# Gate rows spread over four turns and between other pieces, and channel means broadcast by a DMA through DRAM, in a two-layer graph attention kernel

## The chip, the cores and the metric

The kernel runs on one core of one Trainium2 chip. The metric is device time in microseconds (us) of one execution; a kernel's time is the median of its runs. The profile is one execution, recorded by the hardware profiler. Engines are named as the profile does: PE is TensorE, PEld its weight loads, DVE is VectorE, ACT is ScalarE, POOL is GpSimd, SP the queue that issues the DMAs.

## The reference, cut to what matters

Two layers on x of shape (16, 1024, 256). The first (a graph convolution with two batch norms) is untouched by the change. In the second, every one of the 16 batches needs this:

```python
fea = jnp.transpose(x, (0, 2, 1))                       # x: (16, 1024, 256)
c_adj = jnp.mean(fea, axis=1)                           # channel means, one per node: (16, 1024)
diff = c_adj[:, None, :] - c_adj[:, :, None]            # 1024 x 1024 per batch
A = jnp.abs(jnp.abs(jax.nn.sigmoid(diff) - 0.5) - 0.5) * 2.0
A_s = (A + jnp.transpose(A, (0, 2, 1))) * 0.5
Wg = adj[None, :, :] * A_s                              # the gate, times the adjacency matrix
g = jnp.einsum('bcn,bnm->bcm', fea, Wg)
g = jax.nn.relu(g * para.reshape(1, C, N))              # becomes the queries, 4 heads of 64
# k, v = x @ kv_w ; attention = softmax(q k^T * scale) v ; then a residual and a layer norm
```

A *gate row* in the kernel is 128 of the 1024 rows of Wg, for all 1024 columns: eight gate rows, 0 to 7, per batch. To make one, ScalarE needs the means of all 1024 nodes along the free axis, the same in every partition. That tile is called `crow`.

## The kernel before: the parts that matter

The attention phase is a software pipeline over batches. While batch b-1 is in attention, the keys, values, gate rows and graph product of batch b are made, and the input of batch b+1 is normalised. One batch of attention is eight *turns*; a turn has two steps of scores, exponentials and attention matmuls, and a list of other pieces of work. `at` says which pieces belong to a turn, and `arrange` puts them in order. Every engine works in its program order.

```python
ps_s = pool("ps_s", 2, space=PSUM)     # PSUM holds TensorE's results; scores: two tiles
ps_t = pool("ps_t", 3, space=PSUM)     # everything else: three tiles
...
def crow(b, h):                        # the means of a batch, spread over all partitions, in two halves
    if h == 0:
        crows[b] = crp.tile([P, N], F32, tag="crow", name=f"crow_{b}")
    p = ps_t.tile([P, FB], F32, tag="t", name="pc")
    for k in range(FB // P):
        j = h * (FB // P) + k
        nc.tensor.transpose(p[:, ts(k, P)], css[b][:, j : j + 1].to_broadcast([P, P]), ident)
    nc.scalar.copy(crows[b][:, ts(h, FB)], p)

def wg_a(b, i):                        # gate row i: an odd one is one ScalarE pass, an even one two
    t = wgp.tile([P, N], F32, tag="wg", name=f"wg_{b}_{i}")
    wgs[b, i] = t
    if i % 2:
        nc.scalar.activation(t, crows[b], AF.Tanh, bias=hcs[b][:, i : i + 1], scale=-0.5)
        ti = t.bitcast(mybir.dt.int32)
        nc.vector.tensor_scalar(ti, ti, -(2**31), None, op0=OP.bitwise_or)
    else:
        nc.scalar.activation(t, crows[b], AF.Abs, bias=css[b][:, i : i + 1], scale=-1.0)
        nc.scalar.activation(t, t, AF.Tanh, scale=-0.5)

def wg_b(b, i):                        # VectorE: times the adjacency row
    t = wgs[b, i]
    nc.vector.scalar_tensor_tensor(t, t, 1.0, adj_sb[:, i, :], op0=OP.add, op1=OP.mult)
...
WG = (3, 3, 1, 1)                      # gate rows made in turns one to four
...
def arrange(pieces):
    few = sorted((fa for fa in pieces if fa[0] not in long), key=lambda fa: rank.get(fa[0], 11))
    many = [fa for fa in pieces if fa[0] in long]        # keys, values, graph: TensorE's long pieces
    ...                                                  # gate rows have the last rank: they stand together,
                                                         # behind the turn's other short pieces
for t in ...:                          # one turn (cut)
    scores(g + 2); exps(g + 2)
    ...
    sums(g)                            # VectorE adds up the exponentials, for the softmax denominators
    for f, a in now:                   # the turn's other pieces, arranged
        f(*a)
    sums(g + 1)
    scores(g + 3); exps(g + 3)
    attend(g); attend(g + 1)
```

Two more pieces recur below. `finish_a` transposes an output block into a tile `pf` of the pool `ps_t`, and VectorE reads it into a tile `r`, which frees the PSUM tile; that product is "r" in what follows. `values` makes the value projection into a tile `pv` of the same pool.

## Time and profile before

| what | before |
|---|---|
| median of the first three runs (range) | 2753.9 us (2753.35 to 2755.53) |
| a steady batch of the attention phase | 113.03 us |
| TensorE busy in it | 111.25 us |
| ScalarE, VectorE busy in it | 62.17 us, 70.83 us |

One view more: VectorE's order. The columns are start (us), length (us), engine, line, operation, output and inputs, count, and in brackets idle time before and its releaser.

```profile
1353.45 2.48 DVE L521 TENSOR_TENSOR acc<-acc,e 128x1024 f32<-128x1024 f32 x2
1355.84 1.22 DVE L518 TENSOR_TENSOR acc<-e,e 128x1024 f32<-128x1024 f32 x1
1356.98 0.68 DVE L574 TENSOR_TENSOR r<-pf,RD 128x512 f32<-128x512 f32 x1
```

Three additions for the denominators (`acc`, 3.7 us together) stand directly ahead of r, the product that frees the PSUM tile for which a value projection waits until 1357.71.

### The profile page before, as it was taken

The numbers are of one execution on the slowest core, as the hardware profiler recorded it, in microseconds if no ns is written. First come the engines' busy times: TensorE is split into PE (matmuls) and PEld (weight loads), VectorE is DVE, ScalarE is ACT, GpSimd is POOL, SyncE is SP. The second block draws the span as 40 slices with busy tenths as digits, with TensorE's granted clock in tenths as the row PEclk, the third lists the DMA queues.
The fourth block names the chain that finished last, engine by engine and source line by source line (L and its number), as shares of the span: only waits on it lengthen the run. The fifth ranks groups of instructions, "written<-read, shape, count | busy, mean of one in ns | idle before, by whom it ended". The sixth has DMA issues, their size and how long they took to land.

```text
span 2752.7 us, 24565 instructions
## 1 busy us (share of the span) xinstructions
PE 2684.0 (98%) x9306; PEld 1153.1 (42%) x9306; DVE 1305.4 (47%) x2089; ACT 1249.2 (45%) x1695; POOL 184.4 (7%) x404
## 2 busy tenths in 40 slices
PE   8999999999999799999999999999999999999997
PEld 4444444444444443444434444444443444444432
DVE  3101101102222555657656566565665756656646
ACT  2111111112555554654645546456464564645634
POOL 0000000000000100001001010010100100001002
PEclk9999999999999899999999999999999999999999
DMA  3212212220682200000100001000100011000000
GB/s 122 77 62 91 80 59 90 82 86 0 212 298 100 89 24 27 24 23 27 43 24 24 23 28 43 23 23 28 38 28 24 24 35 35 24 24 27 12 8 25
DMA packets 90524, 146.89 MB, mean 53 GB/s; under 512 B 7200, under 2 KB 73248, under 8 KB 84256
## 3 DMA queue, kind: packets, MB, share of 16 engines
q1 hardware_dynamic: 90400, 145.26, 15.0%
q8 instruction: 75, 1.23, 0.2%
q14 instruction: 49, 0.40, 0.0%
HBM read 86.52 MB, written 58.72 MB: 53 GB/s over the span
## 4 chain that ended last, share of the span: by engine, by line
PE 90%; DVE 5%; ACT 3%; issue 1%; DMA 0%; POOL 0%; SPq 0%; DVEq 0%; ACTq 0%; POOLq 0%
PE pa L215 16%; PE s L500 16%; PE pg L480 16%; PE o L530 15%; PE po L304 8%; PE ph L228 8%; PE pk L454 4%; PE pv L465 3%; DVE wg L446 1%; PE px L413 1%; PE pd L549 1%; PE py L390 1%; PE pf L571 1%; DVE acc L521 1%; PE pr L560 1%
## 5 line engine op out<-in xcount | busy, mean ns | idle before, releaser
L512 ACT ACTIVATE e<-s 128x1024 f32<-128x1024 f32 x512 | 497.4, 1020 | 599.7 <-PE o L530 351.8
L500 PE MATMUL s<-qT,kT 64*128 64x512 f32 x2048 | 509.7, 616 | 17.4 <-ACT e L512 17.4
L521 DVE TENSOR_TENSOR acc<-acc,e 128x1024 f32<-128x1024 f32 x384 | 469.5, 1223 | 18.6
L480 PE MATMUL pg<-wg,x 128*128 128x512 f32 x1024 | 470.4, 593 | 0.6 <-DVE wg L446 0.6
L530 PE MATMUL o<-e,v 128*64 128x512 f32 x2048 | 467.7, 599 | 0.0
L215 PE MATMUL pa<-AhT,x 128*128 128x512 f32 x1024 | 442.0, 592 | 0.5 <-issue 0.5
L247 DVE BATCH_NORM_STATS2 st<-ph 128x6 f32<-128x512 f32 x128 | 89.4, 698 | 558.6 <-ACT hT L246 558.6
L500 PEld LDWEIGHTS s<-qT,kT 64*128 64x128 f32 x2048 | 175.0, 186 | 327.0 <-issue 192.1
L215 PEld LDWEIGHTS pa<-AhT,x 128*128 128x128 f32 x1024 | 194.7, 190 | 244.9 <-issue 243.7
L530 PEld LDWEIGHTS o<-e,v 128*64 128x64 f32 x2048 | 135.6, 136 | 316.4 <-issue 315.3
L480 PEld LDWEIGHTS pg<-wg,x 128*128 128x128 f32 x1024 | 180.4, 191 | 160.4 <-issue 159.0
L228 PE MATMUL ph<-agg,W1T 128*128 128x512 f32 x512 | 222.2, 592 | 0.0
L222 ACT COPY agg<-pa 128x512 f32<-128x512 f32 x64 | 37.4, 585 | 404.7 <-PE pa L215 404.7
L446 DVE SCALAR_TENSOR_TENSOR wg<-wg,adj_sb 128x1024 f32<-128x1024 f32 x128 | 156.8, 1225 | 77.5 <-ACT wg L442 74.0
L304 PE MATMUL po<-hL,W2T 128*128 128x512 f32 x384 | 165.0, 592 | 0.0
L518 DVE TENSOR_TENSOR acc<-e,e 128x1024 f32<-128x1024 f32 x64 | 78.2, 1221 | 153.1 <-PE pd L549 153.1
L228 PEld LDWEIGHTS ph<-agg,W1T 128*128 128x128 f32 x512 | 97.4, 190 | 122.3 <-issue 122.1
L485 DVE TENSOR_TENSOR qT<-pg,para_sb 128x512 f32<-128x512 f32 x64 | 44.2, 690 | 204.3 <-PE pg L480 204.3
L246 ACT COPY hT<-ph 128x512 f32<-128x512 f32 x128 | 74.9, 585 | 144.9 <-PE ph L228 144.9
L465 PE MATMUL pv<-kvw,x1T 128*128 128x256 f32 x512 | 119.4, 382 | 6.6 <-DVE r L574 6.6
L308 DVE BATCH_NORM_STATS2 st<-po 128x6 f32<-128x512 f32 x64 | 44.7, 698 | 169.4 <-PE po L304 169.4
L454 PE MATMUL pk<-x1T,kvw 128*128 128x512 f32 x256 | 117.3, 601 | 1.0 <-ACT kT L457 1.0
(106 smaller groups left out, 1990.6 us busy)
## 6 DMA issues: line engine op xcount, KB each, us to landing
h<-hT SPq DMA_DIRECT2D x24, 1024.0 KB, 3.8
hL<-h SPq DMA_DIRECT2D x24, 1024.0 KB, 6.3
x<-in_x_dram SPq DMA_DIRECT2D x16, 1024.0 KB, 5.1
yT<-y SPq DMA_DIRECT2D x32, 512.0 KB, 3.7
yt<-yT SPq DMA_DIRECT2D x64, 256.0 KB, 3.5
xr<-in_x_dram SPq DMA_DIRECT2D x64, 256.0 KB, 3.6
out_dram<-r SPq DMA_DIRECT2D x64, 256.0 KB, 2.1
A<-in_adj_dram SPq DMA_DIRECT2D x4, 1024.0 KB, 8.1
```

The source lines that it names most:

```text
L215: nc.tensor.matmul(p, xts[b][:, k, ts(c, P)], AhT[:, k, ts(h, FB)], start=(k == 0), stop=(k == NT - 1),)
L228: nc.tensor.matmul(p, W1T[:, k, ts(f, P)], aggT[b][:, k, ts(h, FB)], start=(k == 0), stop=(k == CT - 1),)
L247: nc.vector.bn_stats(st1[:, f, u, :], p)
L304: nc.tensor.matmul(po[c], W2T[:, k, ts(c, P)], hT[u][:, k, :], start=(k == 0), stop=(k == HT - 1))
L446: nc.vector.scalar_tensor_tensor(t, t, 1.0, adj_sb[:, i, :], op0=OP.add, op1=OP.mult)
L454: nc.tensor.matmul(p, kvw[:, k, ts(c, P)], x1Ts[b][:, k, ts(h, FB)], start=(k == 0), stop=(k == CT - 1))
L465: nc.tensor.matmul(p[:, ts(a, C)], x1Ts[b][:, k, ts(j + a, P)], kvw[:, k, C:], start=(k == 0), stop=(k == CT - 1),)
L480: nc.tensor.matmul(pg[b], x1s[b, k // 2][:, k % 2, ts(c, P)], wgs[b, k][:, ts(h, FB)], start=(k == 0), stop=(k == NT - 1))
L500: nc.tensor.matmul(t[:, h, :], kTs[b, pair][h * HD : (h + 1) * HD, ts(cb, P)], qTs[b, pair, hf][h * HD : (h + 1) * HD, :], start=True, sto ...
L512: nc.scalar.activation(E[g, a], S.pop((g, a)), AF.Exp)
L521: nc.vector.tensor_add(ACC[b, hf, pair], ACC[b, hf, pair], E[g, a])
L530: nc.tensor.matmul(O[b, hf, pair][h * HD : (h + 1) * HD, :], vs[b][:, cb, pair * P + h * HD : pair * P + (h + 1) * HD], E[g, a][:, h, :], ...
```

## The change

Its intent is threefold. First, seven of a batch's eight broadcast transposes leave TensorE: one transpose, a 4 KB store and a DMA that reads the stored row into all 128 partitions do the same. Second, gate rows are made two per turn. Third, they no longer stand in one block but row by row (a row is a pair of pieces, `wg_a` and `wg_b`) between others. The rest of `arrange` also moves other pieces: in the second turn the pf transposes go behind the first value projection. The core of the diff:

```diff
+    c_dram = [dram.tile([NT, P], F32, name=f"crow_d{b}") for b in range(B)]
-        def crow(b, h):
+        def crow(b):
             ...                                    # batch 0 keeps the eight transposes
+            nc.tensor.transpose(p[:NT, :P], css[b], ident)
+            t = crows[b][:NT, :P]
+            nc.scalar.copy(t, p[:NT, :P])
+            nc.sync.dma_start(c_dram[b], t)
+            nc.sync.dma_start(crows[b], c_dram[b].rearrange("j p -> (j p)").partition_broadcast(P))
-        WG = (3, 3, 1, 1)
+        WG = (2, 2, 2, 2)
         def arrange(pieces):
+            first = [fa for fa in pieces if fa[0] is dens]
+            gate = [fa for fa in pieces if fa[0] in (wg_a, wg_b)]
             ...                                    # "order": the other pieces, short between long
+            pairs = [gate[k : k + 2] for k in range(0, len(gate), 2)]
+            res = spread(order, pairs) if order else pairs
             ...
+            return first + flat
```

More of the change, by code (lines that the diff above doesn't have):

```diff
@@ L419, in means @@
             nc.vector.tensor_scalar_mul(hcs[b], css[b], 0.5)
-        def crow(b, h):
-            if h == 0:
-                crows[b] = crp.tile([P, N], F32, tag="crow", name=f"crow_{b}")
-            p = ps_t.tile([P, FB], F32, tag="t", name="pc")
-            for k in range(FB // P):
-                j = h * (FB // P) + k
-                nc.tensor.transpose(p[:, ts(k, P)], css[b][:, j : j + 1].to_broadcast([P, P]), ident)
-            nc.scalar.copy(crows[b][:, ts(h, FB)], p)
+        def crow(b):
+            crows[b] = crp.tile([P, N], F32, tag="crow", name=f"crow_{b}")
+            if b == 0:
+                for h in range(NH):
+                    p = ps_t.tile([P, FB], F32, tag="t", name="pc")
+                    for k in range(FB // P):
+                        j = h * (FB // P) + k
+                        nc.tensor.transpose(p[:, ts(k, P)], css[b][:, j : j + 1].to_broadcast([P, P]), ident)
+                    nc.scalar.copy(crows[b][:, ts(h, FB)], p)
+                return
+            p = ps_t.tile([P, FB], F32, tag="t", name="pc")
+            nc.tensor.transpose(p[:NT, :P], css[b], ident)
[3 more added lines that the diff above has]
+            nc.sync.dma_start(crows[b], c_dram[b].rearrange("j p -> (j p)").partition_broadcast(P))
         def wg_a(b, i):
@@ L653, in fast @@
             put(b - 2, NC - 2, means, b)
-            for h in range(NH):
-                put(b - 2, NC - 1, crow, b, h)
+            put(b - 2, NC - 1, crow, b)
             i = 0
@@ L683, in fast, with spread @@
         long = (keys, values, graph)
+        def spread(few, many):
+            res, done = [], 0
+            for k, fa in enumerate(few):
+                upto = len(many) * (k + 1) // (len(few) + 1)
+                res += many[done:upto] + [fa]
+                done = upto
+            return res + many[done:]
         def arrange(pieces):
-            few = sorted((fa for fa in pieces if fa[0] not in long), key=lambda fa: rank.get(fa[0], 11))
+            first = [fa for fa in pieces if fa[0] is dens]
+            gate = [fa for fa in pieces if fa[0] in (wg_a, wg_b)]
             many = [fa for fa in pieces if fa[0] in long]
-            n = sum(f in short for f, _ in few)
-            res, k, done = [], 0, 0
-            for f, a in few:
-                res.append((f, a))
-                if f in short and f is not dens:
-                    k += 1
-                    upto = len(many) * k // n
-                    res += many[done:upto]
-                    done = upto
-            return res + many[done:]
+            few = [fa for fa in pieces if fa not in first + gate + many]
+            few.sort(key=lambda fa: rank.get(fa[0], len(rank)))
+            few_pe = [fa for fa in few if fa[0] in short]
+            order = spread(many, few_pe) if len(many) < len(few_pe) else spread(few_pe, many)
+            if few_pe and many and order[0][0] in long:
+                order.remove(few_pe[0])
+                order.insert(0, few_pe[0])
+            for fa in few:
+                if fa[0] not in short:
+                    at_ = 0
+                    for k, o in enumerate(order):
+                        if o[0] in rank and rank[o[0]] <= rank.get(fa[0], len(rank)):
+                            at_ = k + 1
+                    order.insert(at_, fa)
+            pairs = [gate[k : k + 2] for k in range(0, len(gate), 2)]
+            res = spread(order, pairs) if order else pairs
+            flat = []
+            for o in res:
+                flat += o if isinstance(o, list) else [o]
+            return first + flat
         for t in range(min(at), max(max(at), nsteps // 2 - 1) + 1):
```

## The prediction

> **What bounds the kernel now.** I read the page's first part, then the waits of TensorE, then busy time in stretches of one batch, then the order in time of TensorE, ScalarE and VectorE through one batch. The change touches only the attention phase, from about 931 us on.
>
> ```profile
> span 2752.7 us, 24565 instructions
> ...
> PE 2684.0 (98%) x9306; PEld 1153.1 (42%) x9306; DVE 1305.4 (47%) x2089; ACT 1249.2 (45%) x1695; POOL 184.4 (7%) x404
> ...
> 1326.07:1439.10 113.03, 111.25 (x454) 46.65 (x448) 70.83 (x112) 62.17 (x81) 10.27 (x24) 1.00 0.09 28
> ...
> PE s L500 <- ACT e L512: 17.4, 16, 1.3
> PE px L413 <- DVE x L399: 9.6, 5, 3.3
> PE pat L170 <- DVE A L159: 6.6, 2, 6.3
> PE pv L465 <- DVE r L574: 6.6, 13, 0.5
> ```
>
> TensorE is busy 98% of the span. In the steady state a batch takes 113.03 us, TensorE works for 111.25 of it at full clock, VectorE for 70.83 and ScalarE for 62.17. So a change pays in two ways only: less work on TensorE, or less of the 1.78 us in which it stands still. The waits (engine, tile, releaser; total us, times, longest) say which: score matmuls waiting for an exponential (17.4 us in all) and value projections waiting for a VectorE product (6.6 us, 13 times). The next view shows where they sit in a batch (start, length, count, and the idle time before in brackets).
>
> ```profile
> 1347.48 3.65 PE L530 MATMUL o<-e,v 128*64 128x512 f32 x16
> 1352.41 2.04 PE L500 MATMUL s<-qT,kT 64*128 64x512 f32 x8 [1.27 <-ACT e L512]
> 1354.38 0.66 PE L571 MATMUL pf<-ident,ot 128*128 128x128 f32 x4
> ...
> 1356.61 0.60 PE L390 MATMUL py<-ident,yt 128*128 128x128 f32 x4
> 1357.71 2.00 PE L465 MATMUL pv<-kvw,x1T 128*128 128x256 f32 x8 [0.51 <-DVE r L574]
> ```
>
> Both stalls come once per batch, at the same place, the third of a batch's eight turns; the same two lines recur every 113.03 us from 1126 to 2483 us, so in 13 batches. Measured by starts they cost a little more: an attention group normally hands over after 3.59 us (so at 1351.07, not 1352.41: 1.34 us lost), and a py group after 0.44 us (at 1357.05, not 1357.71: 0.66 lost). Now what ScalarE and VectorE did just before:
>
> ```profile
> 1347.15 1.14 ACT L437 ACTIVATE wg<-crow,hcs 128x1024 f32<-128x1024 f32 x1
> 1348.18 1.14 ACT L441 ACTIVATE wg<-crow,cs 128x1024 f32<-128x1024 f32 x1
> 1349.35 1.06 ACT L442 ACTIVATE wg<-wg 128x1024 f32<-128x1024 f32 x1
> 1350.32 1.13 ACT L437 ACTIVATE wg<-crow,hcs 128x1024 f32<-128x1024 f32 x1
> 1351.36 1.92 ACT L512 ACTIVATE e<-s 128x1024 f32<-128x1024 f32 x2
> ```
>
> Four ScalarE passes of gate rows (an even row is two passes, an odd one is one) stand in one block ahead of the exponentials of scores that were ready at about 1346.7. That block is the first stall. The second is on VectorE: the product r that frees the PSUM buffer stands behind gate products and sums and starts at 1356.98.
>
> **What the Trainium skill says.** "Perfetto Trace Analysis", Identifying the Most-Contended Engine: matmul busy time does not show the distance to the roofline. The trace agrees: the matmul records of a pg group last 593 ns on average, but 12 of them start within 5.25 us, so I count spacings of starts. The same page, Optimization Strategy: a gap that repeats can mean too few buffers for the next tile. It fits here: scores wait for one of two, the value projection for one of three PSUM tiles. "TensorE: Matmul & The Clock Gate", Part 4: PE-mode transpose: about 275 ns for a 128x128 transpose inside a kernel. The pc records last 272 ns, yet four in a row take 0.44 us, so the cost on the path is 0.109 us each. "DMA: Bandwidth & Descriptors", Two DMAs through the same engine are not ordered: a DMA reading what an earlier one wrote must wait for its completion semaphore. So the new pair takes two full flights in series; the built program does have that wait, on the issuing queue.
>
> **The change, part by part.**
>
> *Channel means.* Before, a batch has 8 broadcast transposes and two ScalarE copies (0.585 us each). After, for batches 1 to 15 there is one transpose (128 by 8 in, 8 by 128 out), one small copy and two DMAs; batch 0 keeps the old way. TensorE saves 7 x 0.109 = 0.76 us a batch, and all of it is on the path, because the transposes lie among pg matmuls without idle time: 15 x 0.76 = 11.4 us. ScalarE saves about 0.9 us a batch where it idles anyway. The flight: pc stays at the same place (after px and four pg, 1312.9 in this batch), the copy is done by about 1313.9; 256 KB stores land in 2.1 us and 256 KB loads in 3.5 us (medians of the DMA issues), plus 0.6 us to issue each. An estimate for the 4 KB store and the 512 KB spread is therefore 7 to 8 us: in place at about 1321.5. The first gate row needs it at about 1329.1. Hidden, with some 8 us to spare.
>
> *Gate rows.* They go from 3, 3, 1, 1 a turn to 2, 2, 2, 2, and between other pieces. The work is the same. From the order of the built program and this trace's durations I worked out the third turn anew. TensorE is unchanged up to 1341.58, then pv (1.77), pf (0.43), pv (1.77), scores at 1345.56 as before. ScalarE: first v copy at 1343.5, row 2 from 1344.0 to 1346.2, two yt passes to 1347.2, v copy to 1347.6, row 3 to 1348.7, exponentials 1348.7 to 1350.6. The first ends at 1349.7, before 1351.07, so the score stall goes: 1.34 us a batch.
>
> VectorE: row 2's product can start only at 1346.3, when ScalarE has it. In order: product 1.2, then r and its statistics 2.6 (to 1350.05), row 3's sign bits and product 1.87, two sums 2.39, a first sum 1.14 (to 1355.45), then the r for the second stall, ending 1356.13. TensorE, 1.34 us earlier now, would want that buffer at 1355.64. So about 0.54 us of the 0.66 stays: the same wait, seen against an earlier TensorE. Gain 0.1 us.
>
> I followed the later turns the same way. Turn four now has three ScalarE passes where it had one; ScalarE had been idle there for 4.60 us, and the exponential still ends 3 us ahead of the scores that need it. Row 7's product ends at about 1374.4 and is needed after 1380. The sums that the denominators need end 1.7 us ahead. Turns five to eight have only small swaps. I find no new stall.
>
> *Sum.* Transposes 15 x 0.76 = 11.4; score stall 13 x 1.34 = 17.4, and 0.3 once in the batch before last; second stall 13 x 0.1 = 1.3. Together 30.4 us: 2753.9 - 30.4 = 2723.5 us, a steady batch of 110.8 us in place of 113.03. The filling stretch (931 to 985 us), where ScalarE's rows partly set the pace, comes out within half a microsecond by the same working.
>
> **The rivals.**
>
> First: the spread moves the wait to VectorE. The gate products now stand ahead of r in both turns, and whatever ScalarE is late by is passed on. For it: my own sum leaves only 0.5 us between stall and no stall. If the stall vanishes, 13 x 0.54 = 7 us more are gained: 2716. If VectorE's row runs 0.7 us later than I have it, 9 us are lost: 2733.
>
> Second: the DMA is late and ScalarE, which works in order, stands before the first gate row, holding back the exponentials behind it. Against: 8 us to spare, DMA engines busy 9% of a batch. It takes a flight of over 15 us to begin to hurt; each microsecond beyond the slack of the exponentials would cost up to 15 us in total. A flight of 18 us would eat the whole gain: about 2755.
>
> Third: the stalls are no loss, since what follows catches up. Then only the transposes count: 2742. Against: in the batch shown every other group starts at the earliest moment that the group before allows, so nothing has slack to catch up with.
>
> **Range and chances.** Working on TensorE is counted to a tenth of a microsecond and the score stall has 1.3 us of margin, so the centre is firm; the spread comes from the second stall (-7 to +9), some 3 us in the filling stretch and a small chance of a late DMA. I predict 2723 us, 2713 to 2738 at 8 in 10. A gain above 2% needs 55 us, more than both stalls and all the pc transposes together (40 us): 2%. A loss above 2% needs a new stall of over 5 us in each batch: 2%. Within 2%: 96%.
>
> **What would show it.** A steady batch of 110.8 us with TensorE busy about 110.3. The waits of TensorE: scores on exponentials under 2 us in total instead of 17.4; value projections on r at about 0.4 us, 13 times. pc matmuls 8 + 15 = 23 instead of 128, no ScalarE idle time that ends in the spread DMA, and that DMA landing in 3 to 5 us. I am wrong in a step if scores still wait in the third turn (ScalarE's order), if gate rows wait for a DMA (second rival), if a graph matmul waits for a gate product in turn four or five (the even spread is too late), or if the batch shortens by less than 0.7 us although both stalls are gone (third rival).

## The result, and the profile after

The median after is 2720.74 us (2719.65 to 2721.5, four runs) against 2754.15 us (2753.35 to 2755.53, four runs) before in the same rounds. A ratio here is the mean time of one kernel's fast runs over that of the other's of the same rounds, so not quite the ratio of the medians: 0.9878, with a 95% interval of 0.9861 to 0.9895. The change gains 33.4 us by the medians, 1.2%, within the 2% that count as the same. The prediction said 2723 us, 2713 to 2738.

The busy times from the page of the kernel after:

```profile
PE 2668.9 (98%) x9201; PEld 1140.7 (42%) x9201; DVE 1302.6 (48%) x2089; ACT 1239.2 (46%) x1680; POOL 255.8 (9%) x404
```

TensorE runs 105 matmuls fewer, which is 7 for each of batches 1 to 15. GpSimd's busy time is a surprise: the same 404 instructions take 255.8 us instead of 184.4.

Next, one steady batch, from one pc transpose to the next. The columns are length of the stretch, then busy time (and count) of PE, PEld, DVE, ACT and POOL, the granted clock, the DMA share and GB/s.

```profile
1308.08:1418.67 110.59, 110.35 (x442) 45.96 (x441) 70.60 (x112) 61.53 (x79) 15.33 (x24) 1.00 0.10 34
```

The batch is 2.44 us shorter than the 113.03 before; TensorE stands still for 0.24 us in it instead of 1.78. The waits of TensorE (engine, tile, line, releaser: total us, times, longest) say where the 0.24 is:

```profile
PE pv L475 <- DVE r L584: 3.1, 13, 0.2
...
PE s L510 <- ACT e L522: 0.5, 2, 0.3
```

The wait for exponentials went from 17.4 us to 0.5, and the one for r from 6.6 us to 3.1, still once in each of 13 batches. The same place of the batch in order of time, on TensorE:

```profile
1340.15 3.65 PE L540 MATMUL o<-e,v 128*64 128x512 f32 x16
1343.74 1.99 PE L510 MATMUL s<-qT,kT 64*128 64x512 f32 x8
1345.66 0.66 PE L581 MATMUL pf<-ident,ot 128*128 128x128 f32 x4
...
1347.88 0.60 PE L391 MATMUL py<-ident,yt 128*128 128x128 f32 x4
1348.71 1.99 PE L475 MATMUL pv<-kvw,x1T 128*128 128x256 f32 x8 [0.24 <-DVE r L584]
```

Scores follow the attention group after 3.59 us, the shortest spacing there is; no bracket stands behind them. The value projection still has one. On ScalarE, just before:

```profile
1336.66 1.15 ACT L451 ACTIVATE wg<-crow,cs 128x1024 f32<-128x1024 f32 x1
1337.84 1.06 ACT L452 ACTIVATE wg<-wg 128x1024 f32<-128x1024 f32 x1
1338.81 1.08 ACT L381 ACTIVATE yt<-yt,t,s 128x256 f32<-128x256 f32 x2
...
1340.26 1.15 ACT L447 ACTIVATE wg<-crow,hcs 128x1024 f32<-128x1024 f32 x1
1341.31 1.91 ACT L522 ACTIVATE e<-s 128x1024 f32<-128x1024 f32 x2
```

Three passes of gate rows instead of four, with the yt passes (they normalise the next batch's input) and a copy between them, and the exponentials begin 2.43 us before the scores that need the first of them (1343.74); in the kernel before, they began 1.05 us before (1351.36 against 1352.41). VectorE, at the same place:

```profile
1338.93 1.23 DVE L456 SCALAR_TENSOR_TENSOR wg<-wg,adj_sb 128x1024 f32<-128x1024 f32 x1 [5.51 <-ACT wg L452]
...
1344.44 2.48 DVE L531 TENSOR_TENSOR acc<-acc,e 128x1024 f32<-128x1024 f32 x2
1346.84 1.22 DVE L528 TENSOR_TENSOR acc<-e,e 128x1024 f32<-128x1024 f32 x1
1347.98 0.68 DVE L584 TENSOR_TENSOR r<-pf,RD 128x512 f32<-128x512 f32 x1
```

The three additions still stand ahead of r. VectorE itself stood idle for 5.51 us earlier in the turn, waiting for ScalarE's second pass of gate row 2.

Last, the flight of the means. One line of TensorE, then two of ScalarE, two of the issuing queue, and the entry of that DMA among the DMA issues (KB each, median us from issue to landing):

```profile
1308.08 0.27 PE L435 MATMUL pc<-ident,cs 128*8 128x128 f32 x1
```

```profile
1308.39 0.25 ACT L437 COPY crow<-pc 8x128 f32<-8x128 f32 x1 [1.59 <-PE pc L435]
...
1321.77 1.15 ACT L451 ACTIVATE wg<-crow,cs 128x1024 f32<-128x1024 f32 x1
```

```profile
1308.66 0.30 SPq L438 DMA_DIRECT2D crow_d<-crow  x1
1309.89 0.35 SPq L439 DMA_DIRECT2D crow<-crow_d  x1
```

```profile
crow<-crow_d SPq DMA_DIRECT2D x15, 512.0 KB, 4.0
```

The transpose starts at 1308.08, the store is issued at 1308.66, the spread 1.23 us later, when the store is done, and it lands some 4.0 us after that, at about 1313.9. The whole flight is 5.8 us from the transpose on, with the median landing. The first gate row reads the tile at 1321.77 and has no bracket that names a DMA: 7.9 us to spare.

A word on turns: both stalls do stand in the third turn, at its first scores and its second value projection. But the gate rows that hold up those scores belong to the second turn (rows 3 to 5 before, rows 2 and 3 after), which the prediction counts in when it works out "the third turn".

### The profile page after: what moved, and what is told of

It reads as the page before. It is cut to its first block, busy times and chain, and to the rows that moved or that the text cites. A ratio compares the mean times of both kernels' runs of the same rounds, so it can differ in the third digit from the quotient of the medians.

```text
span 2717.8 us, 24408 instructions
## 1 busy us (share of the span) xinstructions
PE 2668.9 (98%) x9201; PEld 1140.7 (42%) x9201; DVE 1302.6 (48%) x2089; ACT 1239.2 (46%) x1680; POOL 255.8 (9%) x404
## 4 chain that ended last, share of the span: by engine, by line
PE 90%; DVE 5%; ACT 2%; issue 1%; DMA 0%; POOL 0%; SPq 0%; DVEq 0%; ACTq 0%; POOLq 0%
PE pa L216 16%; PE s L510 16%; PE pg L490 16%; PE o L540 15%; PE po L305 8%; PE ph L229 8%; PE pk L464 4%; PE pv L475 2%; PE px L414 1%; PE pd L559 1%; PE py L391 1%; DVE acc L531 1%; DVE wg L456 1%; DVE r L584 1%; PE pf L581 1%
## 5 line engine op out<-in xcount | busy, mean ns | idle before, releaser
L66 POOL TENSOR_SCALAR rs_z<-mv_z 128x2 f32<-128x2 f32 x64 | 24.0, 375 | 1097.5 <-DVE mv_z L346 1096.5
```

## The experiments

My theory is that of the prediction: the gains are independent of each other, and the DMA is hidden. What the change bundles had to be taken apart, for the result alone can't say whether "evenly" or "between" does it, what is left in the wait for r, or how safe the DMA is. All kernels gave correct results. The kernel before was run beside them each time: 2753.67, 2754.51 and 2755.03 us in the three sets.

| kernel | median us (range) | ratio to before (95%) | steady batch us |
|---|---|---|---|
| after | 2720.74 (2719.65 to 2721.5) | 0.9878 (0.9861 to 0.9895) | 110.59 |
| means only | 2742.78 (2741.8 to 2743.52) | 0.9959 (0.9945 to 0.9973) | 112.27 |
| gate rows only (even and between) | 2732.41 (2730.33 to 2733.22) | 0.992 (0.9907 to 0.9934) | 111.36 |
| even only | 2745.76 (2745.03 to 2749.51) | 0.9971 (0.9958 to 0.9985) | 112.36 |
| between only | 2726.68 (2725.9 to 2727.82) | 0.9902 (0.9887 to 0.9917) | 110.86 |
| means and between, not even | 2715.88 (2714.92 to 2716.24) | 0.9859 (0.9843 to 0.9875) | 110.10 |
| after, one sum later | 2715.25 (2714.24 to 2716.54) | 0.9856 (0.984 to 0.9873) | 110.10 |
| after, 2 round trips more | 2720.03 (2719.38 to 2720.96) | 0.9875 (0.9859 to 0.9892) | as after |
| after, 4 round trips more | 2729.79 (2727.22 to 2732.81) | 0.9905 (0.9889 to 0.9922) | 110.6 to 112.5 |
| after, 5 round trips more | 2765.94 (2761.74 to 2766.75) | 1.0038 (1.0021 to 1.0054) | 112.1 to 116.0 |
| before, rows 4, 4, 0, 0 | 2798.66 (2798.08 to 2799.41) | 1.0159 (1.0142 to 1.0176) | 116.03 |

### The means alone

The kernel before with the new `crow` and nothing else of the change.

```diff
-            for h in range(NH):
-                put(b - 2, NC - 1, crow, b, h)
+            put(b - 2, NC - 1, crow, b)          # crow as in the kernel after
```

> The kernel before with the DMA spread of the channel means alone; gate rows stay 3, 3, 1, 1 in the old order. Theory (each part pays separately): seven transposes of 0.109 us fewer in 15 batches, 11.4 us: about 2742.5 us, a steady batch of 112.27 us, both stalls of the third turn unchanged (1.27 and 0.51 us). Rival (the saved TensorE time is swallowed by a later wait, or the DMA flight costs something): 2754 us or more.

Measured: 2742.78 us, 10.9 us less than before, and a batch of 112.27 us, which is 0.76 less than 113.03. Both stalls are what they were (17.4 us 16 times, 6.6 us 13 times). So the transposes are worth what their spacing of 0.109 us says, not the 0.27 us that each record lasts, and ScalarE's shorter work brings nothing more.

### The gate rows alone

The kernel after with the old eight transposes: the diff's other half.

```diff
-            put(b - 2, NC - 1, crow, b)
+            for h in range(NH):
+                put(b - 2, NC - 1, crow, b, h)  # crow as in the kernel before
```

> The changed kernel with the old way of spreading the means (8 transposes a batch), so even rows and the new order alone. Theory: the two stalls lose 2.00 us a batch before and 0.39 after, so 13 x 1.61 = 21 us plus half a microsecond in the filling stretch: about 2732 us, score wait gone, value-projection wait about 0.24 us. If the parts add up, this gain and that of the means alone together give the 33.4 us of the whole change. Rival (the freed transposes are what lets the stalls close): the score stall stays in part, over 2740 us.

Measured: 2732.41 us, 21.3 us less than before, a batch of 111.36 us; scores wait 0.5 us in all, value projections 3.0 us, 13 times. The two halves give 10.9 + 21.3 = 32.2 us against 33.4 together: within the scatter of the medians they simply add.

### Even alone, and between alone

Now the second half is itself split. First the kernel before with the even numbers and its old `arrange`:

```diff
-        WG = (3, 3, 1, 1)
+        WG = (2, 2, 2, 2)
```

> The kernel before with rows 2, 2, 2, 2 and nothing else; the gate rows still stand in one block at the end of a turn. Theory (what counts is where the block stands ahead of the exponentials): the block of the second turn has three ScalarE passes in place of four, so the score stall falls by one pass, from 1.27 to about 0.25 us; the products of VectorE come late in one block, so the value-projection stall stays or grows to about 0.65 us. Lost by starts 1.1 us a batch in place of 2.0: about 2742 us. Rival (even counts are the whole gain of the gate part): 2732 us, no score stall.

Measured: 2745.76 us, a gain of only 7.9 us, and a batch of 112.36. I had missed a stall. TensorE in a steady batch of this kernel:

```profile
1128.95 2.04 PE L500 MATMUL s<-qT,kT 64*128 64x512 f32 x8 [0.23 <-ACT e L512]
...
1134.26 1.99 PE L465 MATMUL pv<-kvw,x1T 128*128 128x256 f32 x8 [0.51 <-DVE r L574]
...
1141.99 2.04 PE L500 MATMUL s<-qT,kT 64*128 64x512 f32 x8 [0.23 <-ACT e L512]
```

The first stall shrinks from 1.27 to 0.23, as a block of three passes is shorter than one of four. But the next turn now makes rows 4 and 5, three passes in one block as well, and stalls by another 0.23; the wait for r is as before. In the profiled execution the filling of the pipeline was longer too: from its first pc transposes (930.06) to its first scores (980.6) 50.5 us pass, in the kernel before 47.7 (929.62 to 977.32). The granted clock was 0.5 for 6.8 us of it (from 957.0), and 1.00 in the kernel before from 950 on. This execution was the slowest of five (2749.51 us; another took 2748.79, the rest 2745.03 to 2745.76), so the longer filling is not shown for the median.

Then the other way round: the new `arrange` with the old numbers of rows.

```diff
         WG = (3, 3, 1, 1)
         def arrange(pieces):
             ...                                  # as in the kernel after
```

> The kernel before with the new order (gate rows between other pieces) but still 3, 3, 1, 1 rows. Theory: row 3 goes ahead of the first v copy into time in which ScalarE idled, so the exponentials end as early as in the changed kernel (no score stall), and VectorE gets row 3 about 3 us earlier, so that its chain to the product r ends at about 1355.1 where TensorE wants it at 1355.64 (times of the profile before): no second stall either. All 2.0 us a batch gained: 2728 us, better than even rows in the new order (2732). Rival (evenness is needed, five passes in a turn are too many for ScalarE): stalls stay, 2740 us or more.

Measured: 2726.68 us, a gain of 27.0 us, and a batch of 110.86 in which TensorE is busy all the time (columns as for the steady batch above):

```profile
1310.00:1420.86 110.86, 110.86 (x451) 46.66 (x450) 70.69 (x112) 62.63 (x80) 15.27 (x24) 1.00 0.09 29
```

Neither stall is left. So the new order does all of the work (no run moves the gate rows without the other pieces that the new `arrange` moves, so it is tested as a whole), and with it in place the even numbers *cost* 2732.41 - 2726.68 = 5.7 us.

### The means and between, without even

If that holds, the kernel after should get faster by taking its even numbers back.

```diff
-        WG = (2, 2, 2, 2)                        # against the kernel after
+        WG = (3, 3, 1, 1)
```

> The changed kernel with rows 3, 3, 1, 1 in place of 2, 2, 2, 2: means by DMA and the new order. Theory (the new order with the old counts leaves no stall in the steady batch, 2726.7 us measured; the transposes are worth 11.4 us beside it): 2715 us, a steady batch of 110.2 us, some 5 us faster than the changed kernel, TensorE's wait for the product r gone. Rival (the parts share their gain, or the DMA comes later than the first gate row here): 2720 us or more.

Measured: 2715.88 us, about 5 us faster than the kernel after. The wait for r is gone, and TensorE is never idle in a stretch a little longer than a steady batch of 110.10 us (columns as above):

```profile
1300.00:1410.20 110.20, 110.20 (x443) 45.89 (x441) 70.83 (x113) 61.75 (x79) 15.30 (x24) 1.00 0.11 34
```

Why three rows are better here than two can be seen on VectorE of this kernel:

```profile
1337.62 0.69 DVE L449 TENSOR_SCALAR wg<-wg 128x1024 int32<-128x1024 int32 x1 [2.33 <-ACT wg L447]
...
1348.53 0.69 DVE L584 TENSOR_TENSOR r<-pf,RD 128x512 f32<-128x512 f32 x1
```

With 3, 3, 1, 1 the second turn begins with row 3, an odd one, which leaves ScalarE after one pass; with three rows to place, `arrange` also puts it ahead of the first value projection and not behind it. VectorE is idle for 2.33 us instead of 5.51 and starts 7.62 us ahead of the score group that opens the third turn (1345.24 in this kernel) instead of 4.81 (1338.93 against 1343.74). It has a sign pass and a product more to do, 1.9 us, and so reaches r about 0.9 us earlier. The value projection wanted it 0.39 us earlier. In the profiled executions the filling is longer here, 49.4 us against 47.6 in the kernel after, so the total gains less than 13 shorter batches (6.4 us).

### The sum that stands before r

The kernel after, with the first sum of a new accumulator moved behind the first `finish_a` of its turn. If the wait for r is VectorE's order and nothing else, it goes.

```diff
+            late = live and step(g)[3] == 0 and any(f is finish_a for f, _ in now)
-            if live:
+            if live and not late:
                 sums(g)
             ...
             for f, a in now:
                 f(*a)
+                if late and f is finish_a:
+                    sums(g)
+                    late = False
```

> The changed kernel with one VectorE instruction moved: in the third and seventh turn of a batch the first sum of exponentials (1.14 us) goes behind the product r. Theory (the rest of the second stall is VectorE's row of work ahead of r, nothing else): r starts 1.1 us earlier, as soon as the pf transposes are there, the value projections stop waiting, 0.39 us by starts in 13 batches: 2715.6 us. Rival (the buffer is freed late for another reason, or the later sum delays an exponential): 2720 us or more.

Measured: 2715.25 us, a batch of 110.10, no wait for r left. The remaining stall was that one addition of 1.22 us ahead of r; moving it gains about the same 5 us as the row numbers do, by another way. A batch gains 0.49 us and not the 0.39 of the start alone, as the value projection behind the wait also handed over later: after 1.93 us (1348.71 to 1350.64) in the kernel after, after 1.82 (1348.99 to 1350.81) here. Both versions beat both kernels; the kernel after was not run beside them, but one with its batch was (2720.03 us, two round trips more, below). They end at the same batch, 110.10 us, because that is TensorE's own work in it; I did not combine them, for there is no idle time in a steady batch to win.

### How far is the DMA hidden?

The flight is made longer by sending the 4 KB to DRAM and back n times more before the spread; each trip must wait for the one before.

```diff
+            for _ in range(n):                   # n = 2, 4, 5
+                nc.sync.dma_start(c_dram[b], t)
+                nc.sync.dma_start(t, c_dram[b])
             nc.sync.dma_start(c_dram[b], t)
             nc.sync.dma_start(crows[b], c_dram[b].rearrange("j p -> (j p)").partition_broadcast(P))
```

> The changed kernel with the small tile sent to DRAM and back twice more before the spread, which makes the flight longer by an estimated 6 us (1.25 us for a store and some 2 us for a load, each twice). In the changed kernel the spread is in place at about 1314.0 and the first gate row reads it at 1321.8 us: 7.8 us to spare. Theory: hidden, 2720.7 us as the changed kernel. Rival (the spread is already close to the path): 2735 us or more.

> The same with five more round trips, an estimated 16 us: in place at about 1330, 8 us after the first gate row wants it. ScalarE works in order, so the copies and exponentials behind that row wait with it, and the scores that TensorE issues at 1330.1 wait for an exponential that ends some 4 to 5 us late. Theory: about 15 x 4.7 = 70 us lost, 2790 us (2770 to 2800), with a score wait of 4 to 5 us in the second turn. Rival (ScalarE's idle time absorbs a late spread): 2721 us.

> The flight made longer by four round trips. A round trip took 2.5 us in the run with five, so the spread is in place 10 us later than in the changed kernel, some 2.1 us after the first gate row wants it. With five the row waited 4.63 us and TensorE lost 1.66 us a batch, so about 3 us of lateness are absorbed. Theory: ScalarE waits about 2.1 us for the DMA in each of 15 batches, and TensorE's steady batch stays 110.6 us; the filling batch, where the wait was longest (10.0 us), may lose some 5 us: 2721 to 2728 us. Rival (every microsecond that ScalarE waits is lost): about 2752 us.

Measured: with two trips nothing changes (2720.03 us). ScalarE waited for the DMA once, 2.0 us in the first batch, and TensorE lost nothing. With five trips the time is 2765.94 us: worse than before, but 24 us less than the 2790 expected. Two sizes were wrong. A round trip takes 2.5 to 2.7 us, not the 3.2 I had reckoned with: the stores of the first three trips are issued at 1323.78, 1326.48 and 1328.99. And part of the lateness is absorbed. ScalarE in a steady batch of the kernel with five trips, then TensorE in the same batch (1346.83) and in two others:

```profile
1341.62 1.15 ACT L454 ACTIVATE wg<-crow,cs 128x1024 f32<-128x1024 f32 x1 [4.63 <-DMA crow<-crow_d]
```

```profile
1008.40 3.78 PE L513 MATMUL s<-qT,kT 64*128 64x512 f32 x8 [6.85 <-ACT e L525]
...
1346.83 2.04 PE L513 MATMUL s<-qT,kT 64*128 64x512 f32 x8 [1.53 <-ACT e L525]
...
1573.45 3.12 PE L513 MATMUL s<-qT,kT 64*128 64x512 f32 x8 [3.72 <-ACT e L525]
```

ScalarE waits 4.63 us, and TensorE then 1.53 us: the other 3.1 us were the lead that the exponentials had. The line at 1008.40 is from the first batch after filling, where the wait was 6.85 us. The same score group took 3.78 us there instead of 1.99. The granted clock (second from last but one column) around it:

```profile
1005.00:1010.00 5.00, 1.60 (x4) 0.84 (x6) 3.73 (x4) 4.26 (x6) 0.00 (x0) 0.50 0.11 37
```

It is 0.50. A long wait costs twice: the idle time, and slow matmuls after it. Over the whole attention phase of this kernel, the score groups after gaps of 1.40 to 2.60 us all took 2.04 us, and those after 3.07, 3.72 and 6.85 us took 3.30, 3.12 and 3.78. The groups behind those three were slow too: up to the first one that starts at its normal distance, the three gaps cost 1.6, 1.6 and 3.0 us beside the idle time. With four trips (2729.79 us, 9 us more than after, a little above the expected 2721 to 2728) ScalarE's waits (2.1 to 4.8 us in a steady batch, where 2.1 was expected) add up to 54.9 us in 15 batches, and TensorE's to 10.7 us, of which 5.08 in one gap of the first batch; so four fifths are absorbed. The rival, that any lateness goes straight into the time (2752), falls.

### The block of gate rows, larger

The third rival held that stalls are caught up later. Then a larger stall should not show in the time either. So the kernel before got four rows, six ScalarE passes, in each of two turns.

```diff
-        WG = (3, 3, 1, 1)
+        WG = (4, 4, 0, 0)
```

> The kernel before with rows 4, 4, 0, 0: the block of the second turn has six ScalarE passes in place of four, all ahead of the exponentials. Theory (the score stall is the length of that block): it grows by two passes, 2.1 us a batch, from 1.27 to about 3.4 us, and the second stall stays about as it is: 13 x 2.1 = 27 us more, about 2781 us. Rival (the stall comes from the sums that free the exponentials' buffers, not from the block): 2754 us, score stall near 1.3 us.

Measured: 2798.66 us, 43.6 us slower than before, against 2781 expected. The stall in TensorE's order of time is as expected:

```profile
1363.36 3.68 PE L500 MATMUL s<-qT,kT 64*128 64x512 f32 x8 [3.40 <-ACT e L512]
```

It is 3.40 us, against 1.27 before. What I had not expected is the length of the score group after it: 3.68 us instead of 2.04. It recurs in all 13 steady batches, after 3.40 or 3.41 us idle: 3.68 us in the first, 3.19 in the last, where the next group is slow as well (the pf transposes take 1.09 us instead of 0.66). The granted clock during and just behind that group:

```profile
1363.36:1367.10 3.74, 3.74 (x9) 1.27 (x10) 3.71 (x4) 2.37 (x4) 0.00 (x0) 0.54 0.01 2
```

TensorE is busy for all of the 3.74 us and gets 0.54 of its clock. So one batch pays 3.40 - 1.27 = 2.13 us of idle time and 1.64 us of slow matmuls, and wins back the second stall (0.66 by starts), which is hidden behind the first here: 3.1 us worked out, 3.0 us measured (116.03 - 113.03). Nothing is caught up: the third rival falls.

## Why the prediction was right

*What bounds the kernel.* Right. Every gain came from TensorE's own work or its two stalls; ScalarE lost work as well and nothing followed from that.

*The transposes, 11.4 us.* Right: 10.9 us by the medians and 0.76 us a batch when done alone. To count spacings of starts instead of busy time was what made it so.

*The score stall, 1.34 us in each of 13 batches.* Right in size: the wait is 0.5 us in all. The working behind it held to a tenth: set 7.33 us later (the distance of the two profiles here), ScalarE starts row 2 at 1343.99 (1344.0 worked out) and the exponentials at 1348.64 (1348.7), VectorE its product at 1346.26 (1346.3). The prediction gave the gain to the two moves of gate rows together and did not ask which did it. The runs show that only the second did: "between" alone removes all of it, "even" alone leaves two stalls of 0.23 us a batch and one of them in a turn that had none. The prediction's "I find no new stall" holds for the change as a whole, and only because of "between".

*The second stall, of which 0.54 us would stay.* This is the term that was off. Measured by starts, 0.39 us stay (a py group hands over after 0.44 us, at 1348.32; the projection started at 1348.71). The scores of the two kernels stand 7.33 us apart (1351.07 without stall against 1343.74), so r started at 1355.31 in the time of the kernel before, where I had 1355.45: VectorE's row was 0.14 us quicker than the sum of my durations. Over 13 batches that is 1.8 us, most of the 2.3 us between 2723 and 2720.7. Another 0.05 us a batch is the stalled score group itself, which handed over after 1.97 us (1352.41 to 1354.38) and now does after 1.92 (1343.74 to 1345.66). A batch of 110.59 instead of 110.8, with TensorE busy for 110.35 (predicted 110.3), says the same.

*The flight of the DMA.* Hidden, as predicted, but its two ends were wrong. From the store's issue to the landing it took 5.2 us instead of 7 to 8, because the 4 KB store and the wait behind it took 1.2 us; I had reckoned from stores of 256 KB. The spread's landing, 4.0 us, is inside the 3 to 5 predicted. And pc does not stay "at the same place": the new order puts it behind eight pg matmuls instead of four, 1.7 us later. The two errors largely cancel, so that the 7.9 us to spare agree with the 8 predicted is in part luck.

*The filling stretch, within half a microsecond.* Right: from first pc transpose to first scores 47.56 us (928.84 to 976.40), before 47.70.

*The first rival* (the wait moves to VectorE) had the true place of what is left: moving one addition removes it and gains 5.5 us by the medians, where I had estimated 7. *The second rival* (a late DMA) was priced about right in where it begins: with four trips more the flight is about 5.8 + 4 x 2.6 = 16 us and the loss begins to show, 9 us; with five, some 19 us, it is 45 us, where I had said 32 us (2755 against 2723) for 18. Some 6 us of the excess are the slow matmuls behind the three long gaps (1.6, 1.6 and 3.0 us), which the prediction did not know of. *The third* falls twice, by the gate rows alone and by the larger block.

*The sum.* 13 steady batches shorter by 2.44 us are 31.7 us, two more batches without seven transposes 1.5 us: 33.2 us, measured 33.4.

What stays open: GpSimd's longer times. They are 253.9 to 264.5 us in the kernels with "between" and 183.3 to 184.4 us in before, means only and even only. But the old order with rows 4, 4, 0, 0 has 213.9 us, so the new order alone is not the cause. At the second turn, GpSimd of the kernel before and then of the kernel after:

```profile
1345.23 0.71 POOL L68 TENSOR_TENSOR rs_z<-rs_z,mhalf 128x2 f32<-128x2 f32 x1
```

```profile
1343.42 1.68 POOL L68 TENSOR_TENSOR rs_z<-rs_z,mhalf 128x2 f32<-128x2 f32 x1
```

The same instruction takes 0.71 us and then 1.68. In the kernel before, VectorE is idle at that moment (from 1344.84 to 1348.32); in the kernel after it works on a gate product (1343.30 to 1344.53) and then on the sums (from 1344.44 on, shown above). The Trainium skill, "GPSIMD Engine Reference", Specifications, says that GpSimd shares its SBUF interfaces with VectorE and that instructions of VectorE with two SBUF inputs contend. Those two have two such inputs, and the traces agree. I count this instruction (L68, 120 times from 985 us on) in the kernel before: 44 times VectorE is idle beside it or nearly so, and it takes 0.71 or 0.72 us; 33 times gate products, sums or the addition to r cover more than half of it, and it takes 0.93 on average and up to 1.74. In the kernel after there are 3 of the first kind and 62 of the second, with rows 4, 4, 0, 0 29 and 62. So it follows what VectorE does beside it; but spans on GpSimd are rough, and no run here isolates the cause. It costs nothing: no wait of TensorE on GpSimd grew in the attention phase.

## What to carry to other kernels

When the busiest engine is 98% busy, price a change by its spacings of starts and its few recurring stalls, and look which engine's *order* makes each stall: one addition moved past the product that frees a buffer was worth as much here as taking the even row numbers back. Take a bundled change apart before keeping it: one of its three parts cost 5 us that the other two hid. And the small DMA pair in place of TensorE work was free here as long as its flight was shorter than the 13.7 us to its first reader; measure that distance, because beyond it the loss grew fast: 9 us with four round trips more, 45 with five.

## What the Trainium skill lacked or had wrong

- "TensorE: Matmul & The Clock Gate", Why this matters for your kernels, says to avoid idle gaps of TensorE above some 3 us, after which the clock drops to half. From the first scores on the traces agree: with gaps of 3.07, 3.40, 3.72, 5.08 and 6.85 us the granted clock fell to 0.5 for 3.4 us or more, which cost, where it was added up, 1.6 us at 3.07, 3.40 and 3.72 and 3.0 at 6.85 beside the idle time, and after gaps of up to 2.60 us score groups took 2.04 or 2.05 us as usual. In the filling, before the first scores, less was enough: in the kernel "between only" the clock was 0.5 from 943.9 to 947.3, behind an idle stretch of 1.95 us before which four transposes (0.66 us) were all that ran since 940.6. No run isolates what counts there.
- The same page, PE-mode transpose, gives a duration of about 275 ns in one kernel, for bf16. The records here, fp32, agree (272 ns), but what a transpose costs among other matmuls is 0.109 us, as the means alone showed: 0.76 us a batch for seven. The page gives no such spacing for transposes.
- No page that I read has a number for a broadcast from one DRAM row to all partitions: 4 KB read into 512 KB landed 4.0 us after issue (median of 15). Nor, beside its figures for single small transfers, for a store and a load in series: a 4 KB store and the wait behind it took 1.2 us, a store and a load back 2.5 to 2.7 us. Both belong to "DMA: Bandwidth & Descriptors".
